# Carrying scan states into a ring of buffers: one pair per copy instead of three

## The chip, the cores and the metric

The kernel runs on one core of one Trainium2 chip. Its engines run side by side, each with its own queue of instructions: PE (TensorE, matrix products into PSUM), DVE (VectorE), ACT (ScalarE), POOL (GpSimd), and SP, which here issues most DMAs. Engines wait for one another through semaphores. The metric is the device time of one execution in microseconds (us); less is better.

## The reference

Four residual layers work on 8 images of 56 x 56 positions with 192 channels, each after a group normalization:

```python
x = x + toeplitz_mixer(gn(x))      # layer 0: gated, long convolutions along both axes
x = x + window_attention(gn(x))    # layer 1: shifted 7 x 7 windows, 6 heads
x = x + depthwise_conv3x3(gn(x))   # layer 2
x = x + selective_scan(gn(x))      # layer 3
```

The change lies in layer 3. Its core is a linear recurrence for each of 384 inner channels, each of 16 states and each of 4 directions (along rows and along columns, forward and backward), over 3136 positions:

```python
delta = softplus(delta + delta_bias)
dA    = exp(delta * A)               # decay, one per channel, state and position
dBu   = delta * u * B                # what is fed in
h[t]  = dA[t] * h[t-1] + dBu[t]      # the scan
y     = sum over the 16 states of h * C, plus D * u
```

The four directions are added, normalized over channels, gated with silu(z) and projected back to 192 channels.

## The kernel before

Layers 0 to 2 and the preparation of layer 3 (its projections, its depthwise convolution, and delta, B and C) are the "front" of an image (`front`, L944: `gate`, `attention`, `conv2`, `inner`, `steps`). The front of image 0 runs alone. After that, two strands run together: the scans of image b, and the front of the next image in small parts between them.

The scan is cut into chunks of 448 positions: 7 chunks for each of 4 directions ("slots", in the order 2, 3, 0, 1) for each of 8 images, 224 in all. In a chunk there are 3 blocks of 128 channels (d) and 8 groups of 2 states (k), so 24 units of work. Such a unit (i, d, k) is called a pair; `pairs` (L1018) lists all 5376 in order. These are the steps of a pair g:

- inject (L1056, L1059, POOL): the product of delta * u with B is written into one slot of `ring`, a buffer of 6 slots; pair g uses slot g % 6. A slot holds, for each of the two states, 448 positions and one more column for the state with which the run begins.
- initial (L1061, L1066, ACT): the states with which the previous chunk ended, or zeros at the start of a direction, are copied into that extra column. One copy writes three neighbouring slots.
- decay (L1068, L1076, ACT): two exponentials write the decays into `ps_a`, of which PSUM holds two.
- scan (L1080, L1085, DVE): one scan instruction goes over both states. The extra column has a delta of 1e30, so its decay is zero, and the scan starts there afresh with the copied state. For even k the result replaces the ring slot, for odd k it replaces the decays in PSUM (`on_pool`, L1048).
- times_c (L1087, L1091): the product with C gives `hc` (4 buffers); POOL makes it for even k, DVE for odd k.
- keep_state (L1093, L1098, ACT): the last column goes to `state`, where a later copy finds it.
- add_up (L1100, L1106, PE): products with the identity sum `hc` over the states in PSUM. `sums` (L1110, DVE) adds this to the image's `ysum`. `finish` (L951) ends a chunk in the last direction, with ACT, POOL (L981, L988), PE and DVE.

The order on each engine is the order in which the loop at L1256 issues instructions (a manual schedule). Iteration g issues: the injection of pair g+2 (`ahead` is 2); times_c of pair g-1 if POOL makes it; keep_state of g-1; the decays of g+1; every third iteration, `initial` for pairs g+1 to g+3; the scan of g; times_c of g if DVE makes it; loads of B and C for the next chunk, on SP (L1027); parts of the front and of `finish`; add_up of g-2.

How much of the front goes into an iteration is settled while the program is built, by `Parts` (L1121). It keeps an estimated clock for each of POOL, ACT, DVE and PE. `run(engine, cost, after...)` advances a clock; `step` admits the next part of the front if its estimated ACT and PE work ends before a limit taken from the coming scan. So the costs charged for the scan's own steps, 0.19 us for `initial` among them, also decide where the front's parts fall.

The dependences between engines come from overlaps of the tiles that instructions read and write. Two lines carry most of what matters here:

```python
nc.gpsimd.tensor_mul(hs[:, :, tokens(i)[0]], dus[i, d].to_broadcast([128, NG, CH]), bms[i, k])
nc.scalar.copy(in_ring(g, 3)[:, :, :, tokens(i)[1]], src.rearrange("p (q n) -> p q n", n=NG))
```

Of the kernel before, what the change touches and what calls it, by code (L numbers as in the profile page):

```python
# [15 lines left out]
F32 = mybir.dt.float32  # L16
# [11 lines left out]
CH = 448  # L28
NCH = L // CH
# [6 lines left out]
NG = 2  # L36
NP = NS // NG
# [51 lines left out]
def model(ctx: ExitStack, tc: tile.TileContext, a: dict, out: bass.AP):  # L89
    nc = tc.nc  # L90
# [213 lines left out]
    with (  # L304
        ExitStack() as own,
    ):
        wp = own.enter_context(tc.tile_pool(name="w", bufs=1))
# [6 lines left out]
        Dsum = wp.tile([128, ND], F32, name="Dsum")  # L314
        ones = wp.tile([128, 128], F32, name="ones")
        nc.vector.memset(ones, 1.0 / DI)
        zero6 = wp.tile([128, 3 * NG], F32, name="zero6")
        nc.vector.memset(zero6, 0.0)
        slab = wp.tile([128, SLAB], F32, name="slab")
        slab_f = wp.tile([128, SLAB_F], F32, name="slab_f")  # L320

# [34 lines left out]
        for i in range(WS):  # L356
            for u in range(2):
                for j in range(WS):
                    at = (i * 2 + u) * WS + j
# [15 lines left out]
        for cw, dg, dg_d in ((cw2, dg2, dg2_d), (cw3, dg3, dg3_d)):  # L375
            n = cw.shape[1]
# [10 lines left out]
        for pads in (pad2_d, pad3_d):  # L387
            for pad in pads:
                n = CP if pads is pad2_d else 128
# [629 lines left out]
        bms, cms, deltas, dus, xcs, states, hss, das, hcs, yps, xds = ({} for _ in range(11))  # L1019

        def load_bc(i, k):
            b, slot, j = chunks[i]
            for ts, name, r0 in ((bms, "bm", 0), (cms, "cm", NS)):
                ts[i, k] = bcp.tile([128, NG, CH], F32, name=name)
                r = slot % 2 * 32 + r0 + NG * k
                src = bc_d[slot // 2][b][r : r + NG, j * CH : (j + 1) * CH]
                nc.sync.dma_start(out=ts[i, k], in_=src.unsqueeze(0).to_broadcast([128, NG, CH]))  # L1027

        def load_xc(i, d):
            b, slot, j = chunks[i]  # L1030
            t = sp.tile([128, CH], F32, name="xcd", bufs=3)
            nc.sync.dma_start(out=t, in_=xc_d[slot // 2][b][:, d, j * CH : (j + 1) * CH])
            return t

        def load_delta(i):
            b, slot, j = chunks[i]
            delta = deltas[i] = delta2[:, i % 2]
            nc.sync.dma_start(out=delta[:, :, 1 : CH + 1], in_=dl_d[slot][b][:, :, j * CH : (j + 1) * CH])

        def times_x(i, d):  # L1040
            du = dus[i, d] = sp.tile([128, 1, HALF + CH], F32, name="du", bufs=3)[:, :, HALF:]
            nc.gpsimd.tensor_mul(du[:, 0, :], deltas[i][:, d, 1 : CH + 1], xcs.pop((i, d)))  # L1042

        def tokens(i):

            return (slice(0, CH), CH, 0) if chunks[i][1] % 2 else (slice(1, CH + 1), 0, CH)

        def on_pool(d, k):  # L1048
            return k % 2 == 0

        def in_ring(g, n):

            at = 1 + chunks[pairs[g][0]][1] % 2
            return ring[:, g % 6 : g % 6 + n, at : at + NG * (CH + 1)].rearrange("p q (n t) -> p q n t", n=NG)

        def inject(g):  # L1056
            i, d, k = pairs[g]
            hs = hss[g] = in_ring(g, 1)[:, 0]
            nc.gpsimd.tensor_mul(hs[:, :, tokens(i)[0]], dus[i, d].to_broadcast([128, NG, CH]), bms[i, k])  # L1059

        def initial(g):  # L1061

            i, d, k = pairs[g]
            at = NG * (NP * d + k)
            src = zero6 if i % NCH == 0 else states[i - 1].rearrange("p d n -> p (d n)")[:, at : at + 3 * NG]
            nc.scalar.copy(in_ring(g, 3)[:, :, :, tokens(i)[1]], src.rearrange("p (q n) -> p q n", n=NG))  # L1066

        def decay(g):  # L1068
            i, d, k = pairs[g]
# [51 lines left out]
        class Parts:  # L1121
# [8 lines left out]
            def run(self, engine, cost, *after):  # L1130
                self.t[engine] = max(self.t[engine], 0.0, *after) + cost
                return self.t[engine]
# [61 lines left out]
        def drain(work, log=None):  # L1194

            while (next(work, None) if log is None else log_of(work, log)) is not None:
                pass
# [18 lines left out]
        ring = wp2.tile([128, 6, SLOT], F32, name="ring")  # L1216
# [7 lines left out]
        with tc.manual_schedule():  # L1224
            for k in range(NP):
                load_bc(0, k)
            load_delta(0)
            for d in range(ND):
                xcs[0, d] = load_xc(0, d)
                times_x(0, d)  # L1230
            ahead, last = 2, len(pairs) - 1
            parts = Parts()
            run = parts.run

            fed, set_, scanned, taken, summed = ([0.0] * (len(pairs) + ahead + 8) for _ in range(5))

            def feed(g):
                inject(g)
                fed[g] = run("P", 1.78, taken[g - 6] if g > 5 else 0.0)

            def take(g):
                times_c(g)
                after = scanned[g], summed[g - 4] if g > 3 else 0.0
                taken[g] = run("P", 1.78, *after) if on_pool(*pairs[g][1:]) else run("D", 1.09, *after)

            def prepare(g):
                decay(g)
                set_[g] = run("A", 1.3, taken[g - 2] if not on_pool(*pairs[g - 2][1:]) else scanned[g - 2])

            for g in range(ahead):  # L1250
                feed(g)
            initial(0)
            prepare(0)
            ahead_of, b_next = None, 1
            ending, anything = None, dict.fromkeys("ADE", 1e9)
            for g, (i, d, k) in enumerate(pairs):  # L1256
                b, slot, j = chunks[i]
                if ahead_of not in parts.clients and b_next < B:
                    ahead_of = parts.add(front(b_next), "front")
                    b_next += 1  # L1260
                more = i + 1 < len(chunks)
                if more and d == 1 and k == 0:
                    b1, slot1, j1 = chunks[i + 1]
                    while (b1, slot1 // 2, j1) not in made:
                        parts.step(anything, ahead_of)
                    load_delta(i + 1)
                    for e in range(2):
                        xcs[i + 1, e] = load_xc(i + 1, e)
                if more and (d, k) == (2, 0):
                    xcs[i + 1, 2] = load_xc(i + 1, 2)  # L1270
                if more and (d, k) in ((1, 6), (1, 7), (2, 6)):
                    times_x(i + 1, k - 6 if d == 1 else 2)
                    run("P", 0.93)
                pi, pd, pk = pairs[g - 1]
                if g + ahead <= last:
                    feed(g + ahead)
                if g and on_pool(pd, pk):
                    take(g - 1)
                if g:
                    keep_state(g - 1)  # L1280
                    run("A", 0.15, scanned[g - 1])
                if g < last:
                    prepare(g + 1)
                if g % 3 == 2 and g < last:
                    initial(g + 1)
                    run("A", 0.19, taken[g - 3])
                scan(g)
                scanned[g] = run("D", 2.02, set_[g], fed[g])
                if not on_pool(d, k):
                    take(g)  # L1290
                if g and pd == ND - 1 and pi + 1 < len(chunks):
                    load_bc(pi + 1, pk)
                done = (i, d - 1) if d else (i - 1, ND - 1)
                if k == 2 and g > NP and chunks[done[0]][1] == 2:
                    xds[done] = load_xc(*done)
                if i % (4 * NCH) == 0 and b > 0 and (d, k) == (1, 4):
                    while ending.at < 3:
                        parts.step(anything, ending)
                if k == 4 and g > NP:
                    sums(*done)  # L1300
                pb, pslot, pj = chunks[i - 1]
                if i and pslot == 1 and (d, k) == (0, 5):
                    while ending in parts.clients:
                        parts.step(anything, ending)
                    ending = parts.add(finish(pb, pj), "finish")

                n1 = max(parts.t["D"], fed[g + 1], set_[g + 1])
                n2 = n1 + (2.02 if on_pool(*pairs[min(g + 1, last)][1:]) else 3.11)
                parts.step({"A": max(n2, fed[g + 2]) - 0.7, "E": n1 + 5.0, "D": 0.2})
                if g >= 2:  # L1310
                    add_up(g - 2)
                    summed[g - 2] = run("E", 1.1, taken[g - 2])
            if on_pool(d, k):
                times_c(last)
            for g in (last - 1, last):
                add_up(g)
            while parts.clients:
                parts.step(anything)
            sums(i, d)
            drain(finish(b, j))  # L1320
# [104 lines left out]
```

## Time and profile before

| | before |
|---|---|
| median of 3 runs | 21627.49 us (21618.97 to 21637.12) |
| profiled execution, its own time | 21638.53 us |
| its span, first to last instruction | 21636.7 us |
| PE busy | 17516.4 us (81%) |
| DVE busy | 15781.2 us (73%) |
| POOL busy | 15086.4 us (70%) |
| ACT busy | 12150.2 us (56%) |
| granted TensorE clock, mean | 0.862 |
| initial copies (L1066) | 1536 from states, 256 from zeros |

The profile is one execution, taken by the hardware profiler. Busy is the time in which an engine executes; waiting for semaphores is not counted. A group of instructions is named by its line, engine, operation and tiles, written as output<-inputs; behind it stand its busy time, the mean duration in ns, and the idle time of the engine just before it with the releaser, the work whose end freed it. A row of waits reads: engine, what waited, what released it, total us, number of waits, longest. In a timeline the first two numbers are start and duration in us, and brackets hold the idle time before. A row of windows gives the busy time of each engine in a stretch, its number of instructions, the clock granted to PE, the busy share of the DMA engines and their rate.

### The profile page before, as it was taken

How to read it: one execution, taken by the hardware profiler on the slowest of the kernel's cores; microseconds unless marked ns; L12 is line 12 of the kernel's file. 1: busy time of each engine (PE TensorE's matmuls, PEld its weight loads, DVE VectorE, ACT ScalarE, POOL GpSimd, SP SyncE). 2: the span in 40 equal slices, each digit the busy share in tenths (PEclk: the TensorE clock that was granted, in tenths of full speed). 3: DMA queues.
4: the chain of work that ended last, by engine and by line, in shares of the span. 5: the costliest groups of instructions: out<-in, count | busy, mean ns of one | idle time of the engine just before them, and what ended most of it. 6: DMA issues, size and time to landing. Idle time of an engine off the chain costs nothing. (4 is left out here: it accounts for less than half of the span.)

```text
span 21636.7 us, 198667 instructions
## 1 busy us (share of the span) xinstructions
PE 17516.4 (81%) x59404; PEld 9109.9 (42%) x59404; DVE 15781.2 (73%) x12469; ACT 12150.2 (56%) x28249; POOL 15086.4 (70%) x9176
## 2 busy tenths in 40 slices
PE   7878678887887788878887888788878888777777
PEld 4845465433443344334433444344433443333333
DVE  2122116986798779967896789778977887788998
ACT  3126113666666666656665667476656665755555
POOL 0000005886788778867886788678877887799998
PEclk9587658988998899888998899889988998888888
DMA  3931676456544655475446654665466546644443
GB/s 87 244 98 39 193 211 176 131 161 211 173 138 145 217 171 148 134 220 174 138 139 206 192 143 126 206 196 146 133 201 195 145 132 189 202 134 132 138 137 115
DMA packets 2566491, 3470.12 MB, mean 160 GB/s; under 512 B 936270, under 2 KB 2518704, under 8 KB 2534578
## 3 DMA queue, kind: packets, MB, share of 16 engines
q1 hardware_dynamic: 2542724, 3340.61, 52.0%
q0 software_dynamic: 15520, 116.14, 1.5%
q8 instruction: 473, 7.75, 0.2%
q14 instruction: 606, 4.96, 0.1%
q10 hardware_dynamic: 7168, 0.65, 0.0%
HBM read 2822.68 MB, written 634.11 MB: 160 GB/s over the span
## 5 line engine op out<-in xcount | busy, mean ns | idle before, releaser
L1106 PE MATMUL ps_y<-hc,ident_sb 128*128 128x448 f32 x21504 | 10046.0, 605 | 966.8 <-POOL hc L1091 957.4
L1059 POOL TENSOR_TENSOR ring<-du,bm 128x896 f32<-128x896 f32 x5376 | 9459.7, 1774 | 1870.1 <-ACT ring L1066 1736.1
L1076 ACT ACTIVATE ps_a<-delta,A_logs_sb 128x449 f32<-128x449 f32 x10752 | 6859.5, 638 | 314.3 <-DVE ring L1085 57.7
L1106 PEld LDWEIGHTS ps_y<-hc,ident_sb 128*128 128x128 f32 x21504 | 4331.0, 211 | 5336.0 <-issue 3600.1
L1085 DVE TENSOR_TENSOR_SCAN ps_a<-ps_a,ring 128x898 f32<-128x898 f32 x2688 | 5429.7, 2020 | 954.6 <-ACT ring L1066 485.6
L1085 DVE TENSOR_TENSOR_SCAN ring<-ps_a,ring 128x898 f32<-128x898 f32 x2688 | 5422.1, 2017 | 488.2 <-ACT state L1098 180.6
L1091 POOL TENSOR_TENSOR hc<-ring,cm 128x896 f32<-128x896 f32 x2688 | 4767.2, 1774 | 898.9 <-DVE ring L1085 497.3
L1091 DVE TENSOR_TENSOR hc<-ps_a,cm 128x896 f32<-128x896 f32 x2688 | 2934.0, 1092 | 950.7 <-PE ps_y L1106 725.3
L1098 ACT COPY state<-ps_a 128x2 f32<-128x2 f32 x2687 | 426.2, 159 | 2932.4 <-DVE hc L1091 2926.2
L287 DVE COPY tzx<-ps_tz 112x448 f32<-112x448 f32 x432 | 269.8, 624 | 1456.4 <-PE ps_tz L281 1261.2
L281 PE MATMUL ps_tz<-tzx,tm 112*112 112x112 f32 x4608 | 1031.4, 405 | 348.6 <-DMA tm<-ext 280.2
L295 POOL DMA_DIRECT2D o<-tzx x192 | 97.3, 513 | 1593.9 <-DVE tzx L287 1510.2
L281 PEld LDWEIGHTS ps_tz<-tzx,tm 112*112 112x112 f32 x4608 | 1021.8, 319 | 389.5 <-issue 385.5
L1098 ACT COPY state<-ring 128x2 f32<-128x2 f32 x2688 | 504.2, 188 | 663.7 <-DVE ring L1085 644.3
L666 PE MATMUL ps_f<-ident_sb,slab 98*98 98x98 f32 x1344 | 333.4, 328 | 628.5 <-ACT slab L659 626.1
L1042 POOL TENSOR_TENSOR du<-delta,xcd 128x448 f32<-128x448 f32 x672 | 659.4, 981 | 19.5 <-DMA slab<-in_w_p_dram 19.4
L83 PE MATMUL ps_f<-slab 96*32 96x448 f32 (+7 forms) x2432 | 604.2, 569 | 71.2 <-DMA slab<-pad 51.5
L1066 ACT COPY ring<-state 128x6 f32<-128x6 f32 x1536 | 292.8, 191 | 629.0 <-POOL ring L1059 627.7
L666 PEld LDWEIGHTS ps_f<-ident_sb,slab 98*98 98x98 f32 x1344 | 205.2, 159 | 1032.7 <-ACT slab L659 813.1
L234 PE MATMUL ps_qv<-wqv,xn 96*128 96x384 f32 (+1 forms) x1200 | 530.1, 525 | 131.1 <-DVE xn L153 67.5
L503 PE MATMUL ps_f<-ident_sb,slab 112*96 112x112 f32 x4704 | 529.1, 267 | 101.0 <-DVE slab L511 53.5
L503 PEld LDWEIGHTS ps_f<-ident_sb,slab 112*96 112x96 f32 x4704 | 506.6, 169 | 240.3 <-issue 105.5
(221 smaller groups left out, 16312.2 us busy)
## 6 DMA issues: line engine op xcount, KB each, us to landing
bm<-bc SPq DMA_DIRECT2D x1792, 448.0 KB
cm<-bc SPq DMA_DIRECT2D x1792, 448.0 KB
xcd<-xc SPq DMA_DIRECT2D x840, 224.0 KB
dl<-slab SPq DMA_DIRECT2D x224, 672.0 KB
delta<-dl SPq DMA_DIRECT2D x224, 672.0 KB
slab<-pad SPq DMA_DIRECT2D x504, 232.0 KB
tzx<-qv SPq DMA_DIRECT2D x192, 588.0 KB
o<-tzx POOLq DMA_DIRECT2D x192, 588.0 KB, 13.8
```

Source lines behind the costliest of these rows:

```text
L83: return f(*args, **kw)
L234: nc.tensor.matmul(pq[:p_t], xn[:CP, 0, tok], wqv[:CP, 0, col], start=True, stop=False)
L281: nc.tensor.matmul(po[:, c, :], t[:, :, c2 + c], x[:, :, c1 + c2 + c], start=True, stop=True)
L503: nc.tensor.matmul(p[:CP, t * TT : (t + 1) * TT], ot[:, n % 2, i, t, c % 2 * CP : c % 2 * CP + CP], ident[:TT, :TT], start=i == 0, stop=i ...
L666: nc.tensor.transpose(p[:PT_, e * PT_ : (e + 1) * PT_], S[:, 3 * g + e, :], ident[:PT_, :PT_])
L1042: nc.gpsimd.tensor_mul(du[:, 0, :], deltas[i][:, d, 1 : CH + 1], xcs.pop((i, d)))
L1059: nc.gpsimd.tensor_mul(hs[:, :, tokens(i)[0]], dus[i, d].to_broadcast([128, NG, CH]), bms[i, k])
L1076: nc.scalar.activation(dA[:, n, :], deltas[i][:, d, at : at + CH + 1], AF.Exp, scale=negA[:, slot, d, c : c + 1])
L1085: nc.vector.tensor_tensor_scan(h, dA, hs, 0.0, ALU.mult, ALU.add)
L1091: (nc.gpsimd if on_pool(d, k) else nc.vector).tensor_mul(hc, h[:, :, tokens(i)[0]], cms[i, k])
L1098: nc.scalar.copy(states[i][:, d, NG * k : NG * k + NG], h[:, :, tokens(i)[2]])
L1106: nc.tensor.matmul(yps[i, d][:, :CH], ident, hcs[g][:, n, :], start=k + n == 0, stop=k + n == NP + NG - 2)
```

## The change

`initial` writes one pair instead of three, and it is called for every pair: in iteration g for pair g+4, after the decays of g+1 and before the scan of g. The first four copies are issued ahead of the first two injections. The planner is charged 0.19 us for every pair instead of every third, not before the time at which it takes times_c of pair g-2 to end. The tile of zeros shrinks from 6 to 2 columns.

```diff
-        zero6 = wp.tile([128, 3 * NG], F32, name="zero6")
-        nc.vector.memset(zero6, 0.0)
+        zero2 = wp.tile([128, NG], F32, name="zero2")
+        nc.vector.memset(zero2, 0.0)
...
-        def in_ring(g, n):
+        def in_ring(g):
             at = 1 + chunks[pairs[g][0]][1] % 2
-            return ring[:, g % 6 : g % 6 + n, at : at + NG * (CH + 1)].rearrange("p q (n t) -> p q n t", n=NG)
+            return ring[:, g % 6, at : at + NG * (CH + 1)].rearrange("p (n t) -> p n t", n=NG)
 
         def inject(g):
             i, d, k = pairs[g]
-            hs = hss[g] = in_ring(g, 1)[:, 0]
+            hs = hss[g] = in_ring(g)
...
         def initial(g):
             i, d, k = pairs[g]
-            at = NG * (NP * d + k)
-            src = zero6 if i % NCH == 0 else states[i - 1].rearrange("p d n -> p (d n)")[:, at : at + 3 * NG]
-            nc.scalar.copy(in_ring(g, 3)[:, :, :, tokens(i)[1]], src.rearrange("p (q n) -> p q n", n=NG))
+            at = NG * k
+            src = zero2 if i % NCH == 0 else states[i - 1][:, d, at : at + NG]
+            nc.scalar.copy(in_ring(g)[:, :, tokens(i)[1]], src)
...
+            for g in range(ahead + 2):
+                initial(g)
             for g in range(ahead):
                 feed(g)
-            initial(0)
             prepare(0)
...
                 if g < last:
                     prepare(g + 1)
-                if g % 3 == 2 and g < last:
-                    initial(g + 1)
-                    run("A", 0.19, taken[g - 3])
+                if g + ahead + 2 <= last:
+                    initial(g + ahead + 2)
+                    run("A", 0.19, taken[g - 2] if g > 1 else 0.0)
                 scan(g)
```

`feed` is the injection with its entry in the planner, `prepare` the decays with theirs.

## The prediction
> **What bounds the kernel now.** I read the page's slices first, then the windows of single stages, then the sums of waits, and last the timeline at one stall. The first 3440 us (products, Toeplitz, the first image's front) hold no instruction of the change, except a start of some microseconds. The scan part runs from 3440 to 21600 us: 5376 pairs, 3.38 us each. It is not one regime:
>
> ```profile
> core 0: us, PE busy (x) PEld busy (x) DVE busy (x) ACT busy (x) POOL busy (x), PEclk, DMA share, GB/s
> 8500.00:9000.00 500.00, 410.34 (x1479) 202.98 (x1478) 471.56 (x391) 358.18 (x1050) 448.68 (x268) 0.91 0.41 126
> 9500.00:10000.00 500.00, 398.94 (x1049) 172.83 (x1048) 340.57 (x218) 355.51 (x639) 365.46 (x219) 0.83 0.66 214
> 20500.00:21000.00 500.00, 362.00 (x726) 156.59 (x725) 467.35 (x296) 264.17 (x606) 492.82 (x296) 0.86 0.38 126
> ```
>
> The first row is a stretch beside attention: DVE is 94% busy and sets the pace. The last is the final part, after the last front: POOL is 98.6% busy and sets it. The middle one lies beside the projections and the steps of the next image: nothing is above 80%, so latency sets it. In the timeline the last softplus of the last front ends near 18870 us. So 4424 pairs run beside a front in 15430 us (3.49 us each) and 952 alone in 2730 us (2.87 us each). Only the mixed part has something to win.
>
> Whole-run sums of waits (engine, line, releaser: us, times, longest):
>
> ```profile
> POOL ring L1059 <- ACT ring L1066: 1736.1, 970, 14.0
> ACT ring L1066 <- POOL ring L1059: 1022.3, 595, 302.1
> PE ps_y L1106 <- POOL hc L1091: 957.4, 485, 14.3
> DVE hc L1091 <- PE ps_y L1106: 725.3, 483, 14.6
> DVE ps_a L1085 <- ACT ring L1066: 485.6, 285, 10.6
> DVE ring L1085 <- ACT ring L1066: 171.5, 77, 12.6
> ```
>
> POOL's injection waits for ACT's copy, ACT's copy waits for POOL's injection, and the scan waits for the copy. The large number, 1736 us, is on POOL; what DVE loses to the copy is 657 us. The window of the mixed part holds 1699 us of the first row, 355 of the second (302 is one wait at the start), 337 of the third and 472 of the last two; the final part has 37 on POOL and 185 on DVE.
>
> Two groups give the costs (busy, mean ns | idle before):
>
> ```profile
> L1066 ACT COPY ring<-state 128x6 f32<-128x6 f32 x1536 | 292.8, 191 | 629.0 <-POOL ring L1059 627.7
> L1098 ACT COPY state<-ring 128x2 f32<-128x2 f32 x2688 | 504.2, 188 | 663.7 <-DVE ring L1085 644.3 <-DVE gn_mr L414 7.3 <-DMA xcd<-xc 0.9
> ```
>
> One stall in the mixed part, while POOL also serves the end of a chunk:
>
> ```profile
> 7981.64 1.31 ACT L1076 ACTIVATE ps_a<-delta,A_logs_sb 128x449 f32<-128x449 f32 x2
> 7981.69 1.37 POOL L981 TENSOR_TENSOR slab_f<-slab_f 128x672 f32<-128x672 f32 x1 [0.62 <-POOL hc L1091]
> 7983.02 0.98 POOL L1042 TENSOR_TENSOR du<-delta,xcd 128x448 f32<-128x448 f32 x1
> 7983.95 1.78 POOL L1059 TENSOR_TENSOR ring<-du,bm 128x896 f32<-128x896 f32 x1
> 7985.76 0.20 ACT L1066 COPY ring<-state 128x6 f32<-128x6 f32 x1 [2.81 <-POOL ring L1059]
> 7986.00 2.04 DVE L1085 TENSOR_TENSOR_SCAN ps_a<-ps_a,ring 128x898 f32<-128x898 f32 x1 [3.42 <-ACT ring L1066]
> ```
>
> The scan's decay was ready at 7982.95 and its own injection earlier still. It starts at 7986.00 because the copy covers three slots and waits for the next pair's injection: 3 us lost to a dependence that no data needs.
>
> **What the skill says.** The Trainium skill's Perfetto Trace Analysis, section Tensor Engine Instruction, calls ACT, DVE and GPSIMD strict FIFO; the trace agrees: behind the waiting copy above, ACT's next instruction starts 0.10 us after it. ScalarE: Activation LUTs, section What ACT_TABLE_LOAD costs, gives 186 ns + 0.833 ns per element for an ACTIVATE with immediates, of which about 93 ns overlap the next; for 2 elements that is an estimated 188 ns. The trace's 128x2 copy takes 188 ns, the 128x6 one 191, and at 7318.95 us a copy's successor starts 0.08 us later. Perfetto Trace Analysis, section Optimizing Scalar/DVE Operations, has both sides of this change: grouping helps a saturated engine, and smaller instructions help where an unsaturated ACT causes bubbles elsewhere. ACT is 56% busy.
>
> **The change, part by part.**
>
> *Waits removed.* The new copy for pair g+4 touches one slot, whose last users were pair g-2's. In the built program every second copy carries a wait on POOL (the multiply by C of an even pair, two pairs back) instead of every one on an injection just issued. All injections now carry a wait on ACT, but for a copy two iterations old; before, every third waited for one of the preceding iteration. I matched each scan of the mixed part that waited for a copy with that copy. In 69 of 230 the copy had itself stood for POOL; the smaller of both waits sums to 137 us: gain 137. In the others (335 us) ACT itself was late (its table loads and wide activations), and the decay would hold the scan instead; only the copy between decay and scan goes, 161 times about 0.09: gain 15.
>
> *POOL earlier.* 1699 us of POOL's idle time go or move: behind a long ACT block POOL next waits for the scan (now 493 us on that row). It counts where PE or DVE wait for POOL. PE waits 337 us for the product on POOL in the mixed part; before 149 us of that POOL had stood for the copy. DVE waits for PE mostly for other reasons (late loads of padded rows, front matmuls), so I take half: gain 75 (0 to 149).
>
> *ACT no longer blocked.* Of 355 us that copies block ACT in the mixed part, 137 are counted. The rest delays front activations and decays queued behind; a quarter reaches DVE: gain 55 (0 to 218).
>
> *Added copies.* 5376 instead of 1792: 3584 more. Most hide under ACT's waits for DVE (2745 us in the mixed part before state copies alone). I followed ACT back from each of the 594 mixed scans that waited for ACT to its last wait for DVE: those chains hold 1449 pairs and 448 copies, so 1001 more copies on a path that DVE feels. At 0.095 us (back to back) that is a loss of 95; bounds 0 and 1001 x 0.188 = 188. Without the cover of ACT's waits all 3584 would cost 340.
>
> *Final part.* POOL is the pace and waits 37 us for copies: gain 15. At the start copies precede the injections, so the table load (1.28 us) and first decays come earlier: gain 3.
>
> *The planner.* Charging 0.19 us per pair instead of per three, it leaves ACT less room: in the built order the first front's last softplus falls at pair 652 instead of 633, and the seventh's at 502 of its image instead of 392. 110 pairs move from the final part into the mixed one. Each front costs (15430 - 4424 x 2.87) / 7 = 390 us over bare pairs; if that stays, moving pairs costs nothing: 0, bounds -70 to +70 (110 x the 0.62 us between both rates). SP's queue keeps its loads; those for B and C wait for POOL and come a little earlier.
>
> Sum: 137 + 15 + 75 + 55 + 15 + 3 - 95 = 205 us. The profiled execution took 21638.5 (span 21636.7, 2 us around it); 21638.5 - 205 = 21433. It stands 11 us over the median, 21627.5, so I predict 21420 (1.0% faster).
>
> **Rivals.** (a) *The stall only moves.* POOL's idle turns into waits for scans, and of the direct 152 us the copies' 95 and the next waits leave some 30: 21600. For it: attention has 42 us of POOL idle in 500 and DVE is full there; ACT's own lateness is the larger part of the waits. Against: stalls like the one shown are DVE's, with nothing else late. (b) *ACT becomes the bound: slower.* Place: ACT's chains around softplus and silu beside the steps. Price: 1001 copies at the full 188 ns lose 188, the longer mixed part loses 70, and of the gains only 137 with half of it taken by the decay remain: 21627 + 258 - 69 = 21816. It decides once more than 300 / 0.095 = about 3160 of 3584 copies, or 1600 at full length, are felt. Against: ACT waits for DVE more than for anything else. (c) *POOL's lateness is the hidden pace.* All 472 us of scan waits and all 337 of PE's go: 21627 - 809 + 95 = 20913; halfway, 21100. For it: 1699 us on an engine with 80% load. Against: scans wait directly for an injection 35 us only.
>
> **How the numbers follow.** Forecast 0.56 (its own range 21250 to 21580), (a) 0.15, (b) 0.13, (c) 0.16. A change under 0.2% (43 us) is about what a measurement cannot tell from none. So faster 0.72, same 0.15, slower 0.13. The range 21100 to 21670 leaves out (b) and the far half of (c).
>
> **What would show it.** Right: POOL's wait for the copy falls below 600 us; copies waiting for POOL below 200; scans waiting for copies below 200, with waits for decays (536 us) up by at most 300; ACT busy up by some 500 us; the final part at 2.85 us a pair. Wrong: scans' waits for decays rising by as much as those for copies fall (a or b), copies standing for POOL's product, or the mixed part slower than 3.49 us a pair.

## The result and the profile after

| | before | after |
|---|---|---|
| median, four runs each, same chip | 21628.6 us | 21489.1 us (21476.96 to 21510.71) |
| ratio to before, with its 95% interval | | 0.9935 (0.9923 to 0.9948) |
| profiled execution, its own time; span | 21638.53; 21636.7 us | 21510.71; 21508.5 us |
| granted TensorE clock, mean | 0.862 | 0.865 |
| copies (L1066) | 1792 | 5376 |

The change is worth 139 us of the median. The profiled execution of after is the slowest of its four, 22 us over their median, so its spans understate the gain a little.

The same questions were put to the trace of after. First, the windows: the row that was shown beside attention, the whole mixed part (from the first scan to the last softplus of the last front) and the whole final part:

```profile
8500.00:9000.00 500.00, 417.71 (x1474) 205.75 (x1473) 466.49 (x387) 360.88 (x1140) 446.27 (x267) 0.90 0.44 129
3424.00:19113.00 15689.00, 13021.65 (x44779) 6363.51 (x44780) 12878.39 (x9851) 10223.83 (x26372) 12601.92 (x7537) 0.90 0.56 168
19113.00:21472.00 2359.00, 1759.66 (x3920) 810.93 (x3918) 2206.56 (x1408) 1349.93 (x3524) 2345.34 (x1416) 0.88 0.43 138
```

The same two windows of before:

```profile
3440.00:18870.00 15430.00, 12834.39 (x44359) 6280.29 (x44360) 12612.12 (x9680) 9785.34 (x23004) 12294.50 (x7362) 0.90 0.56 168
18870.00:21600.00 2730.00, 1986.55 (x4337) 913.80 (x4336) 2472.80 (x1579) 1449.56 (x3312) 2638.42 (x1589) 0.88 0.41 133
```

Beside attention nothing has changed: DVE is 93% busy and sets the pace. In the other rows the column to read is the fifth of the busy times, POOL. In the final part POOL stands idle for 14 of 2359 us after, and for 92 of 2730 us before. Both splits in pairs: 4424 mixed and 952 final before, 4534 and 842 after. To compare like with like I use the last 842 pairs of each kernel, counted in scans: 2437.9 us before, 2352.0 after. That is 86 of the 139 us, in one sixth of the pairs. From the first scan to there, the first 4534 pairs took 15722.8 us before and 15695.0 after: 28 us less in the other five sixths. That is within what one profiled execution differs from another there: split_final_only (below) has the copies and the plan of before in its first 4534 pairs and took 15691.5 us for them.

Sums of waits over the whole run of after, the rows that answer to those of before, and two rows for the decays:

```profile
DVE hc L1091 <- PE ps_y L1106: 808.0, 506, 12.5
PE ps_y L1106 <- POOL hc L1091: 750.6, 423, 5.4
ACT ring L1066 <- POOL hc L1091: 617.2, 375, 4.4
DVE ps_a L1085 <- ACT ps_a L1076: 558.2, 344, 10.3
DVE ring L1085 <- ACT ps_a L1076: 407.1, 151, 4.7
POOL ring L1059 <- ACT ring L1066: 383.2, 317, 8.5
DVE ring L1085 <- ACT ring L1066: 76.5, 32, 4.6
```

The two rows for the decays before:

```profile
DVE ps_a L1085 <- ACT ps_a L1076: 411.1, 243, 7.9
DVE ring L1085 <- ACT ps_a L1076: 125.2, 57, 53.6
```

The waits that the change was aimed at are gone: POOL for the copy 1736 to 383 us, the scans for the copy 657 to 79. But the scans' waits for decays rose from 536 to 965, and DVE's wait for PE ahead of its product with C rose from 725 to 808. PE's wait for POOL's product fell from 957 to 751. The copy itself, now behind POOL's product instead of POOL's injection, costs 179 ns where the one of three pairs cost 191 (group; busy, mean ns | idle before):

```profile
L1066 ACT COPY ring<-state 128x2 f32<-128x2 f32 x4608 | 823.0, 179 | 532.2 <-POOL hc L1091 531.1
```

So two questions stand: what made the final part 86 us faster where I had counted 15, and where the mixed part's gain went.

### The profile page after: what moved, and what is told of

The parts are those of the page before. It is cut to its first block, busy times and chain, and to the rows that moved or that the text cites. A ratio compares the mean times of both kernels' runs of the same rounds, so it can differ in the third digit from the quotient of the medians.

```text
span 21508.5 us, 203992 instructions
## 1 busy us (share of the span) xinstructions
PE 17461.0 (81%) x59404; PEld 9086.2 (42%) x59404; DVE 15779.7 (73%) x12469; ACT 12490.5 (58%) x31833; POOL 15095.0 (70%) x9176
## 5 line engine op out<-in xcount | busy, mean ns | idle before, releaser
L1066 ACT COPY ring<-state 128x2 f32<-128x2 f32 x4608 | 823.0, 179 | 532.2 <-POOL hc L1091 531.1
```

The costliest lines, as they stand in the source:

```text
L1066: nc.scalar.copy(in_ring(g)[:, :, tokens(i)[1]], src)
```

## Where the final part's gain comes from

I split POOL's idle time by releaser, in the last 842 pairs alone. Before:

```profile
POOL ring L1059 <- ACT ring L1066: 32.8, 93, 1.1
POOL slab_f L988 <- ACT slab_f L984: 22.9, 13, 1.8
POOL slab_f L981 <- ACT state L1098: 18.8, 7, 2.7
POOL slab_f L981 <- ACT slab_f L977: 9.0, 6, 1.5
POOL hc L1091 <- DVE ring L1085: 2.2, 2, 1.7
```

After, the same view:

```profile
POOL hc L1091 <- DVE ring L1085: 4.9, 3, 3.5
POOL ring L1059 <- ACT state L1098: 2.7, 1, 2.7
POOL hc L1091 <- PE ps_y L1106: 1.5, 3, 0.9
POOL slab_f L981 <- ACT slab_f L977: 1.0, 4, 0.2
POOL hc L1091 <- issue: 0.7, 2, 0.4
```

The first row is the wait for the copy, which I had seen. The next three, 51 us, are POOL's two steps of `finish` (L981, L988). The page puts them down to ACT's steps of `finish`, and nothing in their names points to the copy. The timeline of before does (POOL, ACT and DVE of one finish, other engines left out, further cuts marked):

```profile
21247.90 1.53 DVE L966 TENSOR_TENSOR slab_f<-ysum,ps_f 128x1344 f32<-128x1344 f32 x1
...
21249.41 1.77 POOL L1091 TENSOR_TENSOR hc<-ring,cm 128x896 f32<-128x896 f32 x1
...
21253.88 1.38 POOL L981 TENSOR_TENSOR slab_f<-slab_f 128x672 f32<-128x672 f32 x1 [2.70 <-ACT state L1098]
...
21255.22 1.77 POOL L1059 TENSOR_TENSOR ring<-du,bm 128x896 f32<-128x896 f32 x1
21257.02 0.20 ACT L1066 COPY ring<-state 128x6 f32<-128x6 f32 x1 [1.83 <-POOL ring L1059]
21257.12 1.50 ACT L984 ACTIVATE slab_f<-slab_f,ln_b_sb,ln_g_sb 128x224 f32<-128x224 f32 x3
21257.26 2.04 DVE L1085 TENSOR_TENSOR_SCAN ps_a<-ps_a,ring 128x898 f32<-128x898 f32 x1 [2.77 <-ACT ring L1066]
...
21258.76 1.38 POOL L988 TENSOR_TENSOR slab_f<-slab_f 128x672 f32<-128x672 f32 x1 [1.77 <-ACT slab_f L984]
```

L981 ends at 21255.26 and ACT could start L984. But the copy of three pairs is ahead of it in ACT's queue, waiting for the injection that POOL has only just begun. L984 starts 0.10 us after the copy, and POOL, whose L988 needs it, stands 1.77 us. POOL waits for ACT, which waits for POOL. (The timeline from which the prediction took its stall has the same: at 7988.02, just behind the lines shown there, L988 starts after 2.29 us of waiting for L984.) The same step after:

```profile
21144.17 1.39 POOL L981 TENSOR_TENSOR slab_f<-slab_f 128x672 f32<-128x672 f32 x1
21144.26 0.19 ACT L1066 COPY ring<-state 128x2 f32<-128x2 f32 x1
...
21145.52 1.78 POOL L1059 TENSOR_TENSOR ring<-du,bm 128x896 f32<-128x896 f32 x1
21145.60 1.50 ACT L984 ACTIVATE slab_f<-slab_f,ln_b_sb,ln_g_sb 128x224 f32<-128x224 f32 x3 [1.15 <-POOL slab_f L981]
...
21147.25 1.38 POOL L988 TENSOR_TENSOR slab_f<-slab_f 128x672 f32<-128x672 f32 x1
```

The copy waits for nothing, L984 runs while POOL injects, and L988 follows without a gap. L981's own stall comes about in another way. It stands at the end of a chain that begins with L966 on DVE and goes over ACT and PE. The same chain in split_final_only (below), which differs from before only in the copies of the last 840 pairs:

```profile
21135.04 1.53 DVE L966 TENSOR_TENSOR slab_f<-ysum,ps_f 128x1344 f32<-128x1344 f32 x1
...
21139.31 1.81 POOL L1091 TENSOR_TENSOR hc<-ring,cm 128x896 f32<-128x896 f32 x1
21141.03 1.42 POOL L981 TENSOR_TENSOR slab_f<-slab_f 128x672 f32<-128x672 f32 x1
```

From L966 to L981 it is 5.98 us before and 5.99 here. What differs is how early L966 comes, measured by POOL's work: POOL's product ahead of L981 ends 3.28 us after the start of L966 before, and 6.08 here. Over the 13 finishes in the last 842 pairs that distance is 3.3 us before and 4.6 to 6.1 here, while the chain takes 4.8 to 6.0 in both. DVE's scans wait for copies of three, which wait for POOL's injections, so DVE comes to L966 too late for POOL. That these waits are what makes L966 late is my reading; that the stall goes when the copies are split, the runs below show.

A chunk of the last direction took 74.4 to 75.7 us before and takes 70.3 to 70.7 after, from one L981 to that of the next chunk. Most chunks of the last image without a finish took 66.1 us and take 65.0, from first scan to first scan. Counted in this way, 53 of the 86 us fall to the 11 chunks that lie wholly beside finishes, and 33 to the other 24; the rows above have 51 us for `finish` and 33 for the copy itself.

## The experiments

Each ratio is to before on the same chip, with its 95% interval; a second median is that of before there. "Last 842" is the time of the last 842 pairs in the profiled execution, from the start of the first of their scans to the start of the last. The diffs show the lines of the loop, with cuts marked; where the place of the copies changes, those ahead of the loop change with it and are not shown.

| kernel | median us | before | ratio | last 842, us |
|---|---|---|---|---|
| after | 21489.1 | 21628.6 | 0.9935 (0.9923 to 0.9948) | 2352.0 |
| copies_old_plan | 21495.5 | 21635.8 | 0.9938 (0.9921 to 0.9955) | 2360.0 |
| old_copies_new_plan | 21590.1 | 21635.8 | 0.9981 (0.9970 to 0.9991) | 2436.5 |
| old_copies_new_plan_again | 21576.3 | 21616.4 | 0.9983 (0.9977 to 0.9990) | 2435.2 |
| split_final_only | 21509.6 | 21609.1 | 0.9958 (0.9943 to 0.9973) | 2351.2 |
| split_mixed_only | 21560.3 | 21616.4 | 0.9975 (0.9965 to 0.9984) | 2432.1 |
| doubled | 21703.7 | 21635.8 | 1.0030 (1.0016 to 1.0044) | 2352.6 |
| no_copies | 21346.1 | 21609.1 | 0.9883 (0.9868 to 0.9897) | 2349.5 |
| single_no_lead | 21441.4 | 21635.8 | 0.9911 (0.9896 to 0.9926) | 2350.1 |
| single_no_lead_again | 21490.9 | 21659.8 | 0.9922 (0.9908 to 0.9936) | 2348.6 |
| two_no_lead | 21436.7 | 21609.1 | 0.9921 (0.9906 to 0.9936) | 2360.6 |
| lead3 | 21523.0 | 21609.1 | 0.9958 (0.9944 to 0.9972) | 2360.9 |
| copy_before_keep | 21616.6 | 21659.8 | 0.9981 (0.9974 to 0.9988) | 2354.0 |

The clock granted to PE is not quite the same in all of them. Its mean over the runs is 0.863 to 0.865 for before on the four chips and 0.865 for after, but 0.861 for doubled and 0.868 for no_copies, and 0.866 for old_copies_new_plan_again against 0.864 for split_mixed_only. Among the 77 runs of before beside these kernels, each compared with the others on its chip, 0.001 more of it goes with some 11 us less. Whether the clock makes the time there or the stalls make the clock, no run tells; so a share of the differences in the mixed part and of the price of a copy may go by way of it. In the final part it is 0.88 both before and after.

**The planner apart from the copies.** The new copies with the old charge (against after), and the old copies with the new charge (against before):

```diff
                     initial(g + ahead + 2)
-                    run("A", 0.19, taken[g - 2] if g > 1 else 0.0)
+                if g % 3 == 2 and g < last:
+                    run("A", 0.19, taken[g - 3])
```

> The changed kernel's copies (one pair, four ahead), but the planner is charged for them as before: 0.19 us in every third iteration. The front's parts then stand where they stood before the change. Theory A (the sum of the prediction: planner neutral) and theory B (in the mixed part the stall only moves to late decays; the gain comes from the final part, where POOL is the pace): 21490 us, within 30. Theory C (the longer fronts cost what the prediction gave as the bound, 70 us): 21420.

```diff
                     initial(g + 1)
-                    run("A", 0.19, taken[g - 3])
+                if g + ahead + 2 <= last:
+                    run("A", 0.19, taken[g - 2] if g > 1 else 0.0)
```

> The kernel before with its copies of three pairs, but the planner charged as in the changed kernel. Theories A and B: 21628 us, within 30, as before. Theory C: 21700.

The new copies give the same with either charge, 0.9938 and 0.9935. The old ones gain 0.19% from the new charge alone, 46 us (below the 21598 to 21658 expected), and 40 us when measured again. So the planner's larger charge is no loss; with the old copies it is a small gain, with the new ones 0.03%, and I found no single row of waits that carries it. The last column shows already that the final part goes with the copies and not with the plan: 2352 and 2360 against 2436 and 2438.

**What a copy costs.** Every copy issued twice, and no copies at all. The latter clears the ring once and leaves out carrying the states from chunk to chunk; its scans take as long, since they cover the same columns.

```diff
                     initial(g + ahead + 2)
+                    initial(g + ahead + 2)
                     run("A", 0.19, taken[g - 2] if g > 1 else 0.0)
```

> The changed kernel with every copy issued twice, planner unchanged: 5376 more copies of 128x2. Prediction's price (28% of the copies are felt, 0.095 us each): 5376 x 0.28 x 0.095 = 143 us more, 21630. All felt at 0.095: 510 more, 22000. If ACT's waits hide copies altogether: 21490. Theory B, with ACT as the late engine in the mixed part, expects 100 to 200 more.

```diff
-            for g in range(ahead + 2):
-                initial(g)
...
                 if g + ahead + 2 <= last:
-                    initial(g + ahead + 2)
                     run("A", 0.19, taken[g - 2] if g > 1 else 0.0)
```

> The changed kernel without any copies of states (the ring is cleared once at the start; each scan then starts from whatever its slot holds, so this leaves part of the computation out). Planner charged as in the changed kernel. If a copy costs the same all along (0.040 us, from the doubled kernel): 21489 - 215 = 21275. If the first 5376 copies hide under ACT's waits and only more would be felt: 21420 or more.

The second 5376 copies cost 205 us by the ratios, 215 by the medians: 0.038 to 0.040 us each, more than the prediction's price (143) and the 100 to 200 of theory B. The first 5376, with all the waits that hang on them, cost 0.52% or 112 us by the ratios, 143 by the medians, which are of two chips: 0.021 to 0.027 each. So one line through doubled and after did not lead to no copies: 21346 us lie between the 21275 and the 21420 named for it. But the second copies are not like the first ones. Doubled, then after:

```profile
20504.88 0.42 ACT L1066 COPY ring<-state 128x2 f32<-128x2 f32 x2 [1.72 <-POOL hc L1091]
20505.20 0.19 ACT L1098 COPY state<-ring 128x2 f32<-128x2 f32 x1
```

```profile
20504.08 0.20 ACT L1066 COPY ring<-state 128x2 f32<-128x2 f32 x1 [0.63 <-POOL hc L1091]
20504.18 0.19 ACT L1098 COPY state<-ring 128x2 f32<-128x2 f32 x1
```

A second copy into the same column starts 0.21 us behind the first, where another instruction follows in 0.10. Doubling adds 978 us to ACT's busy time, 0.18 a copy; the first 5376 add 550 between no_copies and after, 0.10 a copy. Set against that, 20 to 26% of the first copies' time is felt and 21 to 22% of the second ones'. About the same share is hidden, so no growing cost per copy is shown. The last 842 pairs take the same 2350 us in all three: where POOL is the pace, ACT's copies are free, as long as nothing that POOL needs stands behind a waiting one.

Doing without the copies altogether, under the new plan, gains 1.17%, about 253 us. Some 40 of that come from the plan with the old copies, so the copies of three cost about 213 in any way. My forecast of 205 asked for nearly all of it.

The scans' waits with no copies at all:

```profile
DVE hc L1091 <- PE ps_y L1106: 751.1, 468, 12.6
DVE ps_a L1085 <- ACT ps_a L1076: 501.9, 321, 10.7
DVE ring L1085 <- ACT state L1098: 345.0, 117, 4.7
DVE ring L1085 <- ACT ps_a L1076: 108.2, 67, 4.6
```

Scans still stand 955 us for ACT: 610 for decays, and 345 in a row that names the copy of a state out of the ring (181 in before). With no copies in its queue, ACT is late there on its own account. DVE's wait for PE is as long as ever.

**The final part alone, and the mixed part alone.** `split_final_only` is before, planner included, with one-pair copies from pair 4536 on, each directly behind the decays of its pair, without a lead (the second argument of `initial` is the number of pairs):

```diff
+                if g < last and (g >= 4535 or g % 3 == 2):
+                    initial(g + 1, 3 if g < 4535 else 1)
                 if g % 3 == 2 and g < last:
-                    initial(g + 1)
                     run("A", 0.19, taken[g - 3])
```

> The kernel before, front parts in the same places, with one pair per copy (no lead) only from pair 4536 on, the last 840 pairs, most of which run without a front beside them. If POOL is the pace there and the traces' 85 us are caused by the copies: 21545 us, within 30, the last 842 pairs in about 2355 us instead of 2438. If the 85 us come from elsewhere: 21628. The prediction had put the gain of this part at 15: 21613.

`split_mixed_only` is after, planner included, with three pairs per copy from pair 4533 on:

```diff
+                if g % 3 == 2 and 4533 <= g + 1 <= last:
+                    initial(g + 1, 3)
                 if g + ahead + 2 <= last:
-                    initial(g + ahead + 2)
+                    if g + ahead + 2 < 4533:
+                        initial(g + ahead + 2)
```

> The changed kernel (planner included) with one-pair copies four pairs ahead only for pairs 0 to 4532, the part beside the fronts; from pair 4533 on, where POOL is the pace, three pairs per copy as before. Theory 'final part' (most of the change's gain is made after the last front, where the copy of three held up the finish of a chunk, and in the mixed part waits for copies only became waits for decays): the last 842 pairs take 2435 us again, and what is left is the planner's share and little else: ratio to before 0.997 to 0.999, within 0.1% of the old copies under the new planner. The prediction's theory (the removed waits pay in the mixed part): ratio 0.9935 to 0.995, the mixed part at 3.46 us a pair and 80 us or more faster than the old copies under the new planner.

> The kernel of old_copies_new_plan once more beside split_mixed_only on the same chip, so that the two differ only in the copies of pairs 0 to 4532. Ratio to before 0.998 again if its first result stands.

The final part alone brings 0.42%, 91 us by the ratio and 100 by the medians (the time is 35 us below the one named), and 87 us in its last 842 pairs, as expected. The mixed part alone brings, beside the old copies under the same planner on the same chip, 21576.3 - 21560.3 = 16 us. The intervals of both ratios overlap, but run against run on that chip the difference of the means is 15 us, with a 95% interval from 3 to 26: a small gain, and far from the 80 us that the prediction's theory asked for. POOL's waits in the last 842 pairs of split_mixed_only are those of before again (its lines are numbered three or four higher):

```profile
POOL ring L1063 <- ACT ring L1069: 32.7, 91, 1.1
POOL slab_f L988 <- ACT slab_f L984: 22.9, 13, 1.8
POOL slab_f L981 <- ACT state L1101: 15.3, 7, 2.7
POOL slab_f L981 <- ACT slab_f L977: 9.0, 6, 1.5
```

In all three kernels with copies of three pairs there L988 stands 13 times for 22.9 us; in after, copies_old_plan, split_final_only and no_copies that row is gone, and POOL's idle time in the last 842 pairs is 11, 10, 4 and 7 us instead of 86 (before), 89 (old_copies_new_plan) and 83 (split_mixed_only). That settles the final part.

How the 139 us divide depends on the order in which the steps are taken, as the planner's gain and that of the mixed part are not independent. Plan first: 40 for the plan, 16 for the mixed part, and the rest, 0.40% or 86 us, for the final part. Copies first: 91 to 100 for the final part (split_final_only), 0.20% or 43 for the mixed part (from there to copies_old_plan; its interval includes zero), and 0.03% or 6 for the plan. Either way the final part has most of it.

**Lead or split?** One pair per copy, without a lead, and the same again later; two pairs per copy, every second iteration (`initial` writes two slots there); and one pair with a lead of three. The planner is charged as in after in all of them.

```diff
-                if g + ahead + 2 <= last:
-                    initial(g + ahead + 2)
+                if g < last:
+                    initial(g + 1)
```

> One pair per copy without the lead: in iteration g the copy for pair g+1, behind that pair's injection, so no injection waits for a copy, and a copy waits only for the injection that its own scan needs anyway. Planner charged as in the changed kernel. If splitting in threes is what helped: 21490 us, within 30, and POOL's waits for copies are near 0. If the lead is what helped: 21560 or more, with scans waiting for copies that wait for injections.

> The kernel of single_no_lead once more, beside copy_before_keep on the same chip, to compare the two directly. Ratio to before 0.991 again if its first result stands; 0.9935 if its lead over the changed kernel was chance.

```diff
+                if g % 2 == 1 and g < last:
+                    initial(g + 1)
                 if g + ahead + 2 <= last:
-                    initial(g + ahead + 2)
```

> Two pairs per copy (2688 copies), issued behind the injections of both, in odd iterations; planner charged as in the changed kernel. No injection waits for a copy, but a scan still waits for the next pair's injection. If POOL's waits for copies were the harm: 2688 copies fewer than with one pair, at 0.040 us each (215 us for 5376 in the doubled kernel): 21441 - 108 = 21335. If the scan's wait for the next injection was the harm: 21470 or more, with the final part back at 2.87 us a pair.

```diff
-                if g + ahead + 2 <= last:
-                    initial(g + ahead + 2)
+                if g + ahead + 1 <= last:
+                    initial(g + ahead + 1)
```

> The changed kernel with the copies three pairs ahead instead of four; a copy's slot was last used one pair earlier, so ACT should hardly wait for POOL's product. If those waits (617 us on ACT) cost time: about 21450. If the place of the copy doesn't matter once it stands ahead of the injection: 21490. Against the kernel without lead (21441) it also tells whether injections that wait for copies cost something.

The lead brings nothing: without it the kernel is at 0.9911 and 0.9922, at least as fast as after. The two intervals of single_no_lead overlap that of after, so I call it a tie with a leaning; the first time came 19 us below the range named for splitting alone. Its waits (second run):

```profile
DVE ps_a L1085 <- ACT ring L1066: 604.3, 407, 11.3
DVE ring L1085 <- ACT ring L1066: 504.9, 237, 4.7
```

1109 us of waits "for the copy", more than the 657 of before, and yet a faster kernel. Here the copy is the last thing that ACT does for the scan, directly behind its decays, and takes over a wait that after shows as one for decays (965). The name of the row says which of ACT's instructions came last, and not which made it late.

Two pairs per copy is a tie too, at 21437 us, with neither of the times that I had named (21335, or 21470 and more): 2688 copies fewer, but each again waits for the next pair's injection, and its last 842 pairs take 2361, not 2.87 us each. The lead of three missed both of its values as well: at 0.9958 it is slower than no lead, and by 0.23% slower than after, where the intervals just overlap. What stands out is its row of POOL's waits:

```profile
POOL ring L1059 <- ACT ring L1066: 2052.8, 1320, 11.1
```

With a lead of three, the copy stands in ACT's queue behind the decays of one iteration, and the injection of the same pair comes next on POOL: it has to wait for it. With four it is one iteration older (383 us), and without a lead the injection comes first. That the copy and the injection write different columns of the slot doesn't help; the waits exist. That this row is what the lead of three loses by isn't shown: between old_copies_new_plan_again and split_mixed_only some 1140 us of the same row went in the mixed part, for 16 us.

**The copy ahead of the state copy.** Last, a place where ACT waits for DVE anyway:

```diff
+                if g < last:
+                    initial(g + 1)
                 if g:
                     keep_state(g - 1)
...
-                if g + ahead + 2 <= last:
-                    initial(g + ahead + 2)
```

> One pair per copy, for pair g+1, as in single_no_lead, but issued ahead of the copy that keeps the state of pair g-1 instead of behind the decays of g+1, so that ACT meets it while it would wait for the scan of g-1 anyway. The planner is charged as in the changed kernel. Theory 1 (a copy costs what of it lies outside ACT's waits for DVE, and in single_no_lead it stood between the decay and the scan): it goes under the wait for the scan, the scans' waits for copies (1040 us in single_no_lead) fall below 200 and waits for decays take most of their place; time between single_no_lead and the kernel without copies, ratio to before about 0.990 (0.988 to 0.991). Theory 2 (a copy close behind its injection blocks ACT's queue when POOL is late, as the copy of three did): copies waiting for POOL rise above 816 us, decays come late, and the ratio is 0.9935 or more, in the final part too, where POOL is the pace (more than 2365 us for the last 842 pairs).

At 0.9981 it loses three quarters of the gain of single_no_lead_again, on the same chip. Its waits:

```profile
ACT ring L1066 <- POOL ring L1059: 1247.3, 871, 286.3
DVE ps_a L1085 <- ACT ps_a L1076: 806.8, 497, 11.2
DVE ring L1085 <- ACT ps_a L1076: 501.6, 220, 51.7
```

The second theory holds in the mixed part. The copy stands for a late injection (267 us there, 694 in the final part), and now the decays stand behind it. In the mixed part scans wait 1291 us for copies and decays together, against 1104 in single_no_lead_again, 187 more, and that part took 15807 us against 15656 (first scan to the last 842 pairs). In the final part it failed: the last 842 pairs take 2354 us, although the copies wait for POOL longer there than in after (694 us against 474). Nothing that POOL needs comes late by it.

## Why the prediction was right, and where not

The time, 21489.1, lies in the range and in the forecast's own range, with the sign right; 139 of the 205 us came. The reasons are another matter. Most of the gain came from a term that I had put at 15, and the terms that made up most of the forecast hardly came: that their errors, some 71 us too low and 171 too high, left the sum in the range was luck.

- *Final part, +15: wrong, it was +86.* The step that failed is "POOL is the pace and waits 37 us for copies". I took the rows that name the copy and left the L981 and L988 rows, because their releasers were steps of `finish`. What released L988 was held by the copy, one place ahead in ACT's queue; L981 stood because DVE, held by the same copies, came too late with L966. Even the 37 us that I had seen were cut to 15 without a reason; the 24 chunks that do not lie wholly beside a finish gave 33 alone. The "2.85 us a pair" named as a test came out at 2.80. I had also said that only the mixed part has something to win, since POOL was 98.6% busy in the window shown; that window of 500 us holds no chunk of the last direction, and so no finish. Over the final part POOL was idle for 92 us.
- *Waits removed, 137 + 15: right in the row, wrong in the time.* The scans' waits for copies in the mixed part fell from 472 to 76 as forecast, under the 200 named. But waits for decays rose from 536 to 944 there, by 408 where I had allowed 300. That is as much as the waits for copies fell (396), which I had named as a sign of being wrong. The scans' waits for ACT of every name (copies, decays, state) fell from 1189 to 1024 us, by 165. Of that, DVE's next wait took half: 722 to 800 for PE at its product with C. In the end DVE is idle for 2811 us in the mixed part and was for 2818 (the rows of both windows), with 110 pairs more. That is rival (a), the stall only moves, and its 30 us are near what the mixed part gave. It was true of the mixed part, and I had given it to the whole.
- *POOL earlier, +75: wrong.* The wait that I meant fell (PE for POOL's product in the mixed part, 337 to 253), but DVE's wait for PE rose instead of falling. POOL's idle time moved as described: it waits 922 us for scans instead of 497, and 497 for PE instead of 177. Why PE comes no earlier wasn't tried and stays open; front matmuls in its queue are a candidate.
- *ACT no longer blocked, +55: not to be seen apart.* Blocking is real where it precedes the decays, as copy_before_keep shows: 187 us more of scans' waits, and 151 us of time in the mixed part. The mixed part's whole yield was 16 us under the new plan and some 43 under the old one, net of the copies' cost, where these terms sum to 282 - 95 = 187.
- *Added copies, -95: about right.* 3584 copies at the 0.021 to 0.027 us of the first 5376 are 75 to 97. ACT's busy time rose by 340 us, not by 500; that is 3584 times 0.095, so the price back to back was right and the 500 didn't agree with it. The share that is felt, 28% in the prediction, came out at 20 to 26%.
- *Planner, 0: right beside the new copies (6 us), and 40 us off, on the favourable side, beside the old ones*, within the bounds of 70 both times. It did move 110 pairs, as the built order said.
- *Start, +3: can't be told.* The first scan came 16 us earlier, but kernels with any form of copy put it anywhere from 3409 to 3462 us.
- *Other tests.* POOL's wait for the copy fell to 383 (below 600: right). Copies waiting for POOL were to fall below 200: 617, wrong over the whole run, and copies standing for POOL's product were themselves named as a sign of being wrong; 143 of it is in the mixed part, and 474 in the final one, where it costs nothing, as POOL is the pace there. The mixed part was not slower than 3.49: 3.46 us a pair.

Rival (b) did not occur: even with all copies doubled, ACT costs 0.3% over before. Rival (c) is excluded by no_copies: no scan and no injection waits for a copy there, and it still takes 21346 us (0.9883). The "halfway" of (c) was also set wrong: between 21627 and 20913 lies 21270, and not 21100. And the 42 us of POOL idle beside attention that (a) names are its waits for copies alone; the window has 51.

## What to carry over

When the engine that sets the pace waits for an instruction on another engine, look what stood ahead of that instruction in its queue: the row of waits names the last link only, and a small blocked copy shows up under the names of its successors. Idle time of the pacing engine is worth its full length (75 us less of it on POOL in the last 842 pairs, 86 us of time), while in the mixed part removing some 1140 us of POOL's waits paid 16 under the same plan, net of the added copies. So sum the idle of the pacing engine over its whole stretch, not over one clean window; the Trainium skill's Perfetto Trace Analysis, section Optimization Strategy, also has one look for the gaps on the engine that matters in each regime, and what blocks them. Splitting a grouped instruction pays by what its group made it wait for, and by its place in the queue: ahead of the decays it lost three quarters of the gain, behind them it needed no lead. And when two effects are measured one after the other, try the other order before their shares are believed.

## What the hardware showed beside this

The Trainium skill's Perfetto Trace Analysis, section Tensor Engine Instruction, calls ACT a strict FIFO, and these traces agree in all that is shown above (L984 starts 0.10 us behind the blocked copy). Not expected were three things. The size of a copy hardly counts: 2 elements per partition take 179 ns on ACT (188 had been estimated), 4 take 184 (two_no_lead) and 6 take 191 (before), and the next instruction starts 0.08 to 0.10 us behind it. A second copy into the same column, however, starts 0.21 us behind the first. And of the time that copies add to ACT, only a fifth to a quarter is felt, on an engine that is 58% busy: 0.021 to 0.027 us each for the first 5376, 0.038 to 0.040 for the second ones. Least explained is the lead: three pairs are worse than none by 0.4 to 0.5%, and than four by 0.2%, where the intervals just overlap.
